# Four graph layers on 32 graphs: where the third and fourth graph's sums of scores are added up

## The chip, the cores and the metric

The kernel runs on one core of a Trainium2 chip. Its engines run side by side, each with its own queue of instructions in an order fixed at build time: PE (TensorE, matrix products into PSUM), DVE (VectorE), ACT (ScalarE), POOL (GpSimd) and SP, which here only issues transfers. They wait for one another by semaphores. The metric is the device time of one execution in microseconds (us), lower being better.

## The reference, cut to what matters

There are 32 graphs of 512 nodes with 128 features each, and one adjacency matrix (512 x 512, zeros and ones) for all of them. Four layers follow one another; each takes a layernorm with ReLU of x and adds its result to x. The change lies in the first, which per graph computes

```python
x_h = elu(x @ Wi + bi)
a_src = x_h @ We[:H, 0]
a_tgt = x_h @ We[H:, 0]
e = sigmoid(a_tgt[:, :, None] + a_src[:, None, :] + be[0])
e = e * (adj + ALPHA * (1.0 - (adj != 0)))
agg = einsum('bij,bjh->bih', e, x_h)
self_part = x_h * sum(e, axis=-1, keepdims=True)
recv = elu(concatenate([agg, self_part], axis=-1) @ Wn + bn)
out = concatenate([recv, x_h], axis=-1) @ Wm + bm
```

The sum over the last axis of e, here called the sum of scores, is one number for each of the 512 target nodes of a graph. The second layer is a recurrent one with five steps of gates, each with a product by the adjacency; the third multiplies by the adjacency and a weight; the fourth is a Chebyshev-like layer with three products by the adjacency for groups of four graphs.

## The kernel before, in words

A graph is held as four chunks of 128 nodes. In the first layer the scores are kept turned round, source nodes on the 128 partitions and the 512 target nodes along the row, so that they make four tiles `es[0]` to `es[3]`, one for each chunk of sources. ACT makes each as a tanh (line 619), and DVE adds one and multiplies by a mask (line 622). The message product (line 630) contracts each tile with the messages in a PSUM bank, `pn`.

The sum of scores is a sum over all four tiles and, inside a tile, over partitions, and it is wanted on all partitions. There are two ways in the code. For the graphs of the first group (b below G = 4) PE multiplies a matrix of ones (128 x 128, full fp32) with each of the four tiles and accumulates in a bank `ps` (line 637, by the helper `product`, whose matmul stands in line 441). For every later graph GpSimd adds the four tiles in three additions (line 641); ACT casts the sum to the reduced fp32r form, `high` (line 647); DVE forms what the cast left out, `low` (line 648); and PE multiplies ones, in fp32r, with both (line 653), into `ps`. After either way DVE multiplies `ps` with x_h (line 656), the product with the lower half of Wn is accumulated onto `pn`, and an elu, the output products (line 666) and the addition to x (line 461) follow. Then the second layer can begin: a layernorm (lines 473 to 486, with a power on GpSimd in line 478), and five steps (lines 839 to 876) of a product by the adjacency (line 820, split into a high and a low part made in lines 790 and 794), gates (lines 845 to 852) and the update (lines 862 to 866).

Besides the sums, graphs of the first group differ from later ones in how they are turned: they use PE transposes (lines 370 and 604), where later graphs go through DVE and transfers.

What sets the order is a planner, run when the kernel is built. Every operation is registered with an engine, an estimated duration, a due time, and what it reads and writes. `Plan.order` then deals them out as if on a clock: each engine takes the ready operation that is due first, provided that buffers are free and that it is due at most 60 us later than the oldest one not begun. An operation of DVE with two inputs in SBUF (`two=True`) and one of POOL never run at the same time in the plan. The resulting order is written into the queues. So an edit of one operation can move all that is planned after it. In the planner's books a full fp32 product is 0.86 us (`T_MM`), a pass of fp32r 0.23 us (`T_PASS`), an addition on GpSimd 1.6 us. A graph's dues count from `begin(b)`: 0, 14, 28 and 42 us for the first four graphs. The first 18 us are planned apart, up to a branch that chooses between exact and inexact adjacency; this adjacency is exact.

Buffers are in kinds: 36 tiles `f` in SBUF (128 x 512 fp32), 4 of fp32r `q`, 8 banks `b` of PSUM, and others.

Of the kernel before, what the change touches and what calls it, by code (L numbers as in the profile page):

```python
# [41 lines left out]
class Plan:  # L42
# [16 lines left out]
    def op(self, eng, us, due, emit, reads=(), writes=(), two=False, keep=0, result=None,  # L59
           earliest=0.0):  # L60

        o = Op(eng, us, self.RESULT[eng] if result is None else result, emit, two, keep)
        o.earliest = earliest
        for v in reads:
            o.before.add(v.writer)
        for v in writes:
            o.before.update(v.readers)  # L70
            if v.writer:
                o.before.add(v.writer)
            elif v.kind and v.slot is None:
                o.takes.append(v)
        for v in reads:
            v.readers.append(o)
        for v in writes:
            v.writer, v.readers = o, []
        o.vals = [v.whole or v for v in dict.fromkeys([*reads, *writes])]
        for v in o.vals:  # L80
            v.left += 1
        for v in [*reads, *writes, *o.vals]:
            self.vals[v] = True
        o.before -= {o, None}
        o.due = max([due, *(b.due for b in o.before)])
        for b in o.before:
            b.after.append(o)
        self.ops.append(o)
# [124 lines left out]
def tile_four_graph_layers(  # L213
# [30 lines left out]
    G = 4  # L244
# [32 lines left out]
    def at(v):  # L277
        if v.tile is not None:
            return v.tile
        return places[v.kind][v.slot] if v.whole is None else at(v.whole)[:, v.part]  # L280
# [152 lines left out]
    def product(w, src, due, dst=None, start=True, stop=True, blocks=False):  # L433

        dst = dst or Val("b")
        def emit():
            to, of = at(dst), at(src)
            if blocks:
                to = to.rearrange("p (c q i) -> p q c i", c=NC, i=32)
                of = of.rearrange("p (q c i) -> p q c i", c=NC, i=32)  # L440
            nc.tensor.matmul(to, at(w), of, start=start, stop=stop)  # L441
        op("PE", T_MM, due, emit, [src, w], [dst])
        return dst
# [104 lines left out]
    def layer0(b, h, due):  # L548
# [82 lines left out]
                at(pn), at(msg)[:, ts(jc, P)], at(es[jc]), start=jc == 0, stop=False),  # L631
                [msg, es[jc]], [pn])

        if b < G:
            ps = Val("b")
            for jc in range(NC):
                product(ones, es[jc], d, ps, start=jc == 0, stop=jc == NC - 1)
        else:
            sums = [Val("f"), Val("f")]
            def add(dst, a, c):  # L640
                op("POOL", 1.6, d - 10, lambda: nc.gpsimd.tensor_tensor(  # L641
                    at(dst), at(a), at(c), op=ALU.add), [a, c], [dst])
            add(sums[0], es[0], es[1])
            add(sums[1], es[2], es[3])
            add(sums[0], sums[0], sums[1])
            high, low, ps = Val("q"), Val("q"), Val("b")
            op("ACT", T_COPY, d, lambda: nc.scalar.copy(at(high), at(sums[0])), [sums[0]], [high])
            op("DVE", T_VEC, d, lambda: nc.vector.tensor_tensor(
                at(low), at(sums[0]), at(high).bitcast(F32), op=ALU.subtract),
                [sums[0], high], [low], two=True)  # L650
            def total():
                for n, part in enumerate((low, high)):
                    nc.tensor.matmul(at(ps), at(ones_r), at(part), start=n == 0, stop=n == 1)  # L653
            op("PE", 2 * T_PASS, d, total, [high, low, ones_r], [ps])
# [23 lines left out]
    def first_layer(b):  # L678
        h = layernorm(b, begin(b))
        layer0(b, h, begin(b))  # L680
# [316 lines left out]
```

## Time and profile before

| What | Value |
|---|---|
| median of 3 runs | 1689.95 us (1689.92 to 1690.58) |
| the profiled execution | 1689.17 us |
| its span (first to last instruction) | 1687.4 us |
| PE busy | 1667.7 us |
| DVE busy | 1457.7 us |
| ACT busy | 1127.8 us |
| POOL busy | 295.8 us |
| PE's products with ones | 32 records, 25.4 to 81.4 us |
| GpSimd's additions (line 641) | 84, of 1.55 us in the mean, 85.3 to 1384.6 us |
| PE's passes with ones in fp32r (line 653) | 56 records |

How to read it: a line of the profile names the kernel's line, the engine, the instruction, what it writes and reads, the shape and the count. A full fp32 matmul shows as two records; records of PE overlap in time, so their sum exceeds the time that passes. A view of stretches gives each engine's busy time between two moments of the span, then the granted clock, the transfer engines' share and GB/s. A view of waits gives for each pair of instructions the total, the count and the longest. The chain is the work that ended last, followed back from the end; its rows give a start, a duration and the work.

### The profile page before, as it was taken

How to read it: one execution, taken by the hardware profiler on the slowest of the kernel's cores; microseconds unless marked ns; L12 is line 12 of the kernel's file. 1: busy time of each engine (PE TensorE's matmuls, PEld its weight loads, DVE VectorE, ACT ScalarE, POOL GpSimd, SP SyncE). 2: the span in 40 equal slices, each digit the busy share in tenths (PEclk: the TensorE clock that was granted, in tenths of full speed). 3: DMA queues.
4: the chain of work that ended last, by engine and by line, in shares of the span. 5: the costliest groups of instructions: out<-in, count | busy, mean ns of one | idle time of the engine just before them, and what ended most of it. 6: DMA issues, size and time to landing. Idle time of an engine off the chain costs nothing.

```text
span 1687.4 us, 21306 instructions
## 1 busy us (share of the span) xinstructions
PE 1667.7 (99%) x6627; PEld 1076.8 (64%) x6627; DVE 1457.7 (86%) x3325; ACT 1127.8 (67%) x2143; POOL 295.8 (18%) x237
## 2 busy tenths in 40 slices
PE   9999999999999999999999999999999999999998
PEld 7555555656666666666666666666666666666797
DVE  6889999999998898889988898889999988877742
ACT  8777676786776676667776677665777766655541
POOL 2121102212122121222202212202222220000110
PEclk9999999999999999999999999999999999999999
DMA  3213333243333332242332433232333333222201
GB/s 107 62 57 101 94 107 94 78 135 95 101 113 101 101 101 85 84 120 95 105 103 77 112 107 92 90 107 88 118 104 99 97 98 94 82 69 88 83 18 52
DMA packets 266875, 156.57 MB, mean 93 GB/s; under 512 B 75392, under 2 KB 235008, under 8 KB 266752
## 3 DMA queue, kind: packets, MB, share of 16 engines
q1 hardware_dynamic: 266752, 155.12, 31.3%
q8 instruction: 54, 0.88, 0.2%
q14 instruction: 69, 0.57, 0.1%
HBM read 82.25 MB, written 72.81 MB: 92 GB/s over the span
## 4 chain that ended last, share of the span: by engine, by line
PE 89%; DVE 6%; ACT 2%; DMA 1%; issue 1%; SPq 0%; DVEq 0%; ACTq 0%
PE b L441 41%; PE b L820 19%; PE b L910 10%; PE b L901 6%; PE b L630 5%; PE b L666 3%; PE b L567 2%; PE b L883 1%; PE b L300 1%; DVE f L845 1%; DVE f L622 1%; DVE r L794 1%; PE b L653 1%; ACT f L486 1%; DVE f L382 1%
## 5 line engine op out<-in xcount | busy, mean ns | idle before, releaser
L478 POOL TENSOR_TENSOR s<-s,nhalf 128x4 f32<-128x4 f32 x128 | 160.0, 1250 | 884.4 <-DVE s L476 840.9
L430 ACT COPY f<-b 128x512 f32<-128x512 f32 x360 | 208.4, 586 | 158.7 <-PE b L820 107.1
L820 PE MATMUL b<-AQ,r 128*128 128x512 f32 x1024 | 302.5, 437 | 1.3 <-DVE r L794 1.3
L820 PEld LDWEIGHTS b<-AQ,r 128*128 128x128 f32 x1024 | 192.2, 188 | 89.9 <-issue 47.4
L845 DVE TENSOR_TENSOR f<-f,b 128x512 f32<-128x512 f32 x320 | 211.6, 676 | 39.8 <-PE b L441 39.1
L446 ACT ACTIVATE f<-f,b4w 128x512 f32<-128x512 f32 x160 | 115.4, 723 | 163.0 <-DVE f L845 160.5
L382 DVE STREAM_TRANSPOSE f<-f 128x512 f32<-128x512 f32 x244 | 205.2, 844 | 21.8 <-ACT f L486 21.3
L910 PE MATMUL b<-r,A_r 128*128 128x512 f32 x768 | 222.8, 426 | 0.0
L486 ACT ACTIVATE f<-x,s 128x128 f32<-128x128 f32 x512 | 210.8, 491 | 17.3 <-DVE s L481 17.2
L641 POOL TENSOR_TENSOR f<-f,f 128x512 f32<-128x512 f32 x84 | 129.9, 1548 | 427.0 <-DVE f L622 299.0
L441 PE MATMUL b<-f,u5T 128*128 128x512 f32 x320 | 163.4, 595 | 6.0 <-DVE f L852 6.0
L910 PEld LDWEIGHTS b<-r,A_r 128*128 128x128 f32 x768 | 139.4, 189 | 46.6 <-issue 24.4
L441 PE MATMUL b<-f,w4T 128*128 128x512 f32 x320 | 163.1, 593 | 2.5 <-ACT f L430 2.5
L441 PE MATMUL b<-f,u3T 128*128 128x512 f32 x320 | 163.3, 593 | 1.7 <-DVE f L866 1.6
L441 PE MATMUL b<-f,w5T 128*128 128x512 f32 x320 | 162.5, 592 | 0.0
L441 PE MATMUL b<-f,w3T 128*128 128x512 f32 x320 | 162.1, 592 | 0.0
L820 PE MATMUL b<-A_r,r 128*128 128x512 f32 x512 | 151.1, 437 | 0.4 <-DVE r L794 0.4
L901 PEld LDWEIGHTS b<-V,f 128*128 128x128 f32 x1024 | 131.8, 191 | 26.3 <-issue 20.1
L862 DVE TENSOR_TENSOR f<-f,f 128x512 f32<-128x512 f32 x160 | 112.9, 707 | 38.0 <-ACT f L446 37.7
L446 ACT ACTIVATE f<-b,b5w 128x512 f32<-128x512 f32 x160 | 109.1, 683 | 53.3 <-PE b L441 52.9
L794 DVE TENSOR_TENSOR r<-f,r 128x512 fp32r<-128x512 f32 x192 | 138.5, 723 | 6.4 <-ACT r L790 6.2
L446 ACT ACTIVATE f<-f,b3w 128x512 f32<-128x512 f32 x160 | 115.0, 720 | 28.8 <-DVE f L845 27.7
(106 smaller groups left out, 2580.5 us busy)
## 6 DMA issues: line engine op xcount, KB each, us to landing
m<-f SPq DMA_DIRECT2D x244, 256.0 KB, 2.1
f<-m SPq DMA_DIRECT2D x184, 256.0 KB, 2.9
f<-m SPq DMA_DIRECT2D x240, 64.0 KB, 2.3
x<-in_x_dram SPq DMA_DIRECT2D x32, 256.0 KB, 3.3
out_dram<-x SPq DMA_DIRECT2D x32, 256.0 KB, 2.4
f<-d SPq DMA_DIRECT2D x28, 256.0 KB, 5.6
f<-in_adj_dram SPq DMA_DIRECT2D x4, 256.0 KB, 3.8
f<-in_L_gnn_weight_dram SPq DMA_DIRECT2D x2, 224.0 KB, 3.3
```

The lines of the kernel that those rows point to most:

```text
L382: op("DVE", us, due, lambda: nc.vector.transpose(view_out(at(blocks)), view_in(at(src))), [src], [blocks])
L430: op("ACT", us, due, lambda: nc.scalar.copy(at(t), at(src)), [src], [t])
L441: nc.tensor.matmul(to, at(w), of, start=start, stop=stop)
L446: op("ACT", us, due, lambda: nc.scalar.activation(at(dst), at(src), AF.Tanh, bias=at(bias), scale=scale), [src, bias], [dst])
L478: op("POOL", 1.35, due, lambda: nc.gpsimd.tensor_tensor(stat(SCALE), stat(VAR), at(neg_half), op=ALU.pow), [s, neg_half], [s])
L486: nc.scalar.activation(at(h)[:, ts(c, P)], at(X[b])[:, c, :], AF.Relu, bias=stat(SHIFT)[:, c : c + 1], scale=stat(SCALE)[:, c : c + 1],)
L641: op("POOL", 1.6, d - 10, lambda: nc.gpsimd.tensor_tensor(at(dst), at(a), at(c), op=ALU.add), [a, c], [dst])
L794: op("DVE", T_VEC, due, lambda: nc.vector.tensor_tensor(part(lo), whole(), part(hi).bitcast(F32), op=ALU.subtract), [src, hi], [lo], two=two)
L820: nc.tensor.matmul(at(pa), at(part)[:, ts(jc, P)], view(at(columns)[:, jc, :]), start=jc == n == 0, stop=jc == NC - 1 and n == PARTS - 1,)
L845: op("DVE", T_VEC, d, lambda: nc.vector.tensor_tensor(at(s), at(u), at(pg), op=ALU.add), [u, pg], [s])
L901: nc.tensor.matmul(at(pz)[:, ts(i, D)], at(hT[i])[:, ts(ic, P)], at(V[k]), start=i == 0, stop=last and i == G - 1,)
L910: nc.tensor.matmul(at(pz), at(adjT)[:, jc, ts(ic, P)], at(part), start=False, stop=jc == NC - 1 and n == PARTS - 1,)
```

## The change

The condition that chooses between the two ways of summing is altered from `b < G`, with G = 4, to `b < 2`. The first and second graph keep the four fp32 products with ones; the third and fourth (b = 2 and 3) now use GpSimd's three additions, the cast, the subtraction and two fp32r passes. How these two graphs are turned, and everything else in the text of the program, stays as it is; the planner then deals out all operations anew.

```diff
-        if b < G:
+        if b < 2:
             ps = Val("b")
             for jc in range(NC):
                 product(ones, es[jc], d, ps, start=jc == 0, stop=jc == NC - 1)
```

## The prediction

> **What bounds the kernel now.** I read the page's busy shares first, then the busy time by stretches, PE's waits, and the rows of the instructions concerned. The shares:
>
> ```profile
> PE 1667.7 (99%) x6627; PEld 1076.8 (64%) x6627; DVE 1457.7 (86%) x3325; ACT 1127.8 (67%) x2143; POOL 295.8 (18%) x237
> ```
>
> PE is busy 99% of a span of 1687.4 us; DVE comes next. These are averages over unlike stages, so the busy times in stretches (PE, PEld, DVE, ACT, POOL, in us) follow. The products that the change removes lie in the second to fourth line:
>
> ```profile
> 40.00:60.00 20.00, 19.95 (x86) 12.25 (x85) 13.96 (x38) 15.61 (x32) 2.55 (x4) 1.00 0.15 49
> 60.00:80.00 20.00, 20.00 (x75) 11.47 (x74) 17.28 (x46) 15.97 (x31) 4.97 (x8) 1.00 0.24 67
> 80.00:100.00 20.00, 20.00 (x76) 11.93 (x75) 15.10 (x35) 16.42 (x32) 4.86 (x4) 1.00 0.18 54
> ...
> 100.00:200.00 100.00, 98.33 (x331) 56.54 (x330) 94.64 (x189) 70.43 (x128) 16.17 (x12) 1.00 0.30 92
> 200.00:300.00 100.00, 97.44 (x310) 54.90 (x309) 93.61 (x190) 65.91 (x121) 17.64 (x12) 1.00 0.29 91
> 300.00:400.00 100.00, 97.08 (x363) 59.42 (x362) 97.00 (x228) 76.49 (x148) 20.05 (x15) 1.00 0.39 111
> 400.00:500.00 100.00, 99.24 (x397) 64.37 (x396) 97.88 (x239) 72.30 (x142) 21.59 (x17) 1.00 0.36 106
> ```
>
> From 40 to 100 us PE has no gap to speak of and DVE is idle for 60 - 13.96 - 17.28 - 15.10 = 13.7 us. From 100 to 500 us the two are nearly level: PE loses 7.9 us there, and DVE is 94 to 98% busy. What PE waits for in all:
>
> ```profile
> PE b L441 <- DVE f L852: 6.0, 5, 1.8
> PE b L441 <- ACT f L430: 2.5, 3, 1.6
> PE b L820 <- DVE r L794: 1.7, 2, 1.3
> PE b L441 <- DVE f L866: 1.6, 1, 1.6
> PE b L300 <- DVE ones L295: 1.0, 1, 1.0
> PE b L630 <- DVE f L622: 0.6, 1, 0.6
> ```
>
> That is 13.4 us in 13 waits, for DVE and ACT alone, and 8.7 us of it (1.6 + 1.6 + 2.6 + 2.9 us by stretches of 100 us) lies between 0 and 400 us. So the end is set by PE's work, plus what the joint stretch makes PE wait. PE's part in the sums of scores, in its timeline and then in the chain that ended last (start, duration):
>
> ```profile
> 59.27 3.60 PE L441 MATMUL b<-f,ones 128*128 128x512 f32 x8
> ...
> 67.91 1.02 PE L441 MATMUL b<-f,ones 128*128 128x512 f32 x2
> ...
> 81.01 1.02 PE L441 MATMUL b<-f,ones 128*128 128x512 f32 x2
> ```
>
> ```profile
> 118.44 0.47 PE b L653 x2
> 118.91 3.43 PE b L441 x8
> ```
>
> The third graph's four products stand together at 59.27 us, the fourth's are scattered from 67.91 to 82 us (another two stand at 78.44 us); each is two records. Records of PE overlap (3.60 us here), so I take the step from the chain: eight records of such products pass in 3.43 us, 0.86 us a product. The pair of passes that later graphs use takes 0.47 us.
>
> **What the skill says.** "FP8 and Floating Point Precision", TensorE Precision Notes, counts four passes through the array for true fp32. The trace agrees in size: 0.86 us a product against 0.47 / 2 = 0.235 us for one reduced pass. "SBUF — State Buffer", Terms, calls the pair of ports that DVE and GpSimd arbitrate for an exclusive lock held for the whole instruction: the loser blocks fully. The trace agrees. In the DVE and POOL timelines, the scalar-tensor-tensor that usually takes 0.68 us takes 1.77 us beside an addition of GpSimd:
>
> ```profile
> 104.38 1.57 POOL L641 TENSOR_TENSOR f<-f,f 128x512 f32<-128x512 f32 x1 [7.95 <-PE b L441]
> ```
>
> ```profile
> 104.73 1.77 DVE L622 SCALAR_TENSOR_TENSOR f<-f,mask 128x512 f32<-128x512 f32 x1
> ```
>
> "Perfetto Trace Analysis", Identifying the Most-Contended Engine, warns that matmul busy share is a poor measure of the distance to the roofline. Here I use it only for gaps: what counts is that no gap follows the removed products.
>
> **The change part by part.**
>
> *Removed from PE:* 2 graphs x 4 products x 0.86 = 6.9 us. *Added to PE:* 2 graphs x 0.47 = 0.9 us. Net 5.9 us less, all of it on the chain that ended last, since PE has no gap from 60 to 140 us.
>
> *Added to GpSimd:* 6 additions x 1.55 us (mean of the row of line 641) = 9.3 us. POOL is busy 7.5 us of 40 to 80 us and stands idle for 9.85 us ahead of 60.02 us and 14.85 us ahead of 78.65 us. The third graph's scores (line 622) are done at 49.6 us; its additions fit there. The fourth's are made at 65.39, 66.59, 69.60 and 70.80 us; two additions can follow the last of them by 74.5 us. A power of a layernorm (line 478, 1.25 us) can come to stand behind one addition, so up to 1.6 us late, and then DVE's line 481 with it. Line 481 waited 1.4 us for POOL in the whole run, so I take nothing for this. The cover is the planner's dealing with several graphs at once; without it the price is 1.6 us a time.
>
> *Added to ACT:* 2 casts x 0.62 = 1.2 us; ACT is idle for 8.4 us between 40 and 80 us. In 28 graphs the cast (line 647) waited 0.5 us in all for POOL, so little queues behind it.
>
> *Added to DVE:* 2 subtractions x 0.69 = 1.4 us, and the lock. The lock's price: lines 622, 852, 862, 864, 866 and 794 have means 203, 21, 27, 24, 16 and 43 ns over 680 ns; times 128, 4 x 160 and 192 instructions these are 26 + 14 + 8 = 48 us. Put on the 84 additions alone, it is 0.58 us each, so 6 x 0.58 = 3.5 us. Its bounds are nothing (GpSimd falls on instructions that read PSUM) and the whole addition, 9.3 us. I take 3.5, which makes 4.9 us on DVE, between 1.4 and 10.7. It is hidden by DVE's 13.7 us of idleness between 40 and 100 us. But PE, 5.9 us ahead, wants DVE's results that much sooner: 4.9 + 5.9 = 10.8 of 13.7 us are then used, and not all idle time can be used. I charge 1 us to this. If the cover were gone, the whole 4.9 us would be paid.
>
> *The waits of the new path:* cast, subtraction, pair of passes, and line 656 behind them. In 28 graphs line 648 waited 2.2 us for ACT and line 656 3.3 us for PE, 0.2 us a graph, in DVE's queue. Against this, the sum is known earlier: the third graph's last score is done at 49.6 us, while its line 656 ran at 62.9; the fourth's ran at 82.5. Nothing that I see becomes late. *Buffers:* two more of the 36 f buffers a graph for a few us, two of 4 q buffers that were last used for the adjacency casts; and a PSUM bank held about 1.5 us, where the fourth graph held one from 67.9 to 83.2 us. No price, perhaps a small gain. *DMA:* no transfer is added, removed or issued elsewhere on purpose; SP's queue changes only by its order.
>
> *The order:* the planner writes all queues from about the first such addition on anew, with 4 x 0.86 us of PE replaced by 2 x 0.23 in its books, and each addition keeping two-input work of DVE away for 1.6 us. The work after 100 us is the same, in another order, and so meets other waits. PE's loss in stretches of 100 us is 1.7, 2.6, 2.9, 0.8 and 1.6 us between 100 and 600 us, then 0 to 1.5. An estimate from this scatter, about 1 us a stretch over 16 stretches: the sum of 13.4 us can come out 4 us higher or lower. It can't fall below 0, so no more than 5.9 + 13.4 = 19 us can be won.
>
> Sum against the profiled execution (1689.17 us; span 1687.4): 1689.17 - 5.9 + 1.0 = 1684.2. The median of the runs, 1689.95, is 0.8 us above the profiled one, so 1685.0 us.
>
> **The rivals.** 0.2% of 1690 us is 3.4 us, about what a measurement can tell from no change.
>
> *A. Won, as summed.* 1681 to 1686.5 us, at 1685. For it: PE's closed row from 60 to 140 us. Against it: the level race after 100 us.
>
> *B. The gain waits at DVE.* PE comes to the stretch from 100 to 500 us up to 5.9 us early, and DVE can't follow: PE's waits grow from 13.4 to 17 or 19 us. At 146 us PE did wait, and the chain ran over DVE and ACT for 13 us. Time about 1689, between 1686.5 and 1693.3. Against it: DVE's idle time before 100 us, much of it spent waiting for PE, which now comes sooner.
>
> *C. DVE starts the stretch late: slower.* Place: lines 622 and 542 to 866 between 48 and 80 us, held by the lock. Price: up to 10.7 us on DVE, all PE's gain then lost in waits behind it. It decides from the point where the idle time takes up less than 10.7 - 3.4 = 7.3 us at the upper price (less than 1.5 of 4.9 at the middle one). Typical: 5 us unpaid, 1695; worst 1690 + 10.7 = 1700.7. For it: two-input work fills most of DVE's queue from 64 to 71 us. Against it: 13.7 us of idleness.
>
> *D. A luckier order.* Waits fall too: under 1681 us.
>
> That the additions aren't made at all is no case: the branch is taken at build time by graph number.
>
> **How the numbers follow.** A 0.42, D 0.06, B 0.27, C 0.25. Faster by over 0.2% is A and D, 0.48; within it B, 0.27; slower C, 0.25. Likeliest: A, 1685, with its own range 1681 to 1686.5. The range for 8 in 10 leaves out about 0.04 of D under 1679 and a little under half of C, 0.11, over 1696: 1679 to 1696.
>
> **What would show it.** Records of products with ones fall from 32 to 16, line 641 rises from 84 to 90, line 653's records from 56 to 60. PE's share stays at 99% and its waits within 13 +- 4 us, if A holds. B would show waits of PE for DVE between 100 and 500 us some 4 to 6 us longer; C would show DVE busy for more than 52 of the 60 us from 40 to 100 us (46.3 now, 51.2 as summed), and the rows of lines 622 and 852 to 866 longer there. The forecast is wrong if the new order makes PE lose more than 2.5 us over the 13.4, or if DVE's rows before 100 us lengthen by more than 5 us.

## The result, and the profile after

The changed kernel took 1685.13 us in the median of 9 runs (1684.39 to 1687.89), against 1689.95 us before (9 runs, 1689.15 to 1690.65). The ratio is 0.9972, with a 95% interval of 0.9962 to 0.9983: 4.8 us faster. The forecast was 1685.0 us. The profiled execution took 1684.65 us (1689.17 before).

The busy shares of the changed kernel, and then what PE waited for:

```profile
PE 1663.9 (99%) x6615; PEld 1073.5 (64%) x6615; DVE 1467.1 (87%) x3327; ACT 1129.3 (67%) x2145; POOL 308.0 (18%) x243
```

```profile
PE b L441 <- DVE f L852: 6.0, 9, 1.2
PE b L630 <- DVE f L622: 2.7, 2, 2.0
PE b L820 <- DVE r L794: 1.1, 2, 0.7
PE b L653 <- DVE q L648: 1.1, 3, 0.7
PE b L300 <- DVE ones L295: 1.0, 1, 1.0
PE b L441 <- ACT f L430: 0.5, 1, 0.5
```

The waits sum to 12.4 us (13.4 before), inside the 13 +- 4 us of the forecast. PE has 12 records fewer: 16 records of products with ones (two for each of eight products) are gone and 4 passes came. POOL has 6 instructions more, DVE and ACT two each. So far all is as summed. But the waits have moved, as the busy times in stretches show. First before, then after:

```profile
0.00:100.00 100.00, 98.27 (x456) 64.37 (x457) 73.54 (x218) 81.05 (x166) 22.26 (x39) 1.00 0.28 79
100.00:600.00 500.00, 490.47 (x1783) 298.51 (x1782) 471.94 (x1033) 349.28 (x659) 94.88 (x68) 1.00 0.33 99
600.00:1300.00 700.00, 697.68 (x2750) 450.06 (x2749) 628.98 (x1446) 482.49 (x921) 135.60 (x98) 1.00 0.34 100
1300.00:1600.00 300.00, 300.00 (x1141) 191.75 (x1140) 251.78 (x552) 186.48 (x342) 38.63 (x28) 1.00 0.29 86
```

```profile
0.00:100.00 100.00, 94.30 (x446) 61.57 (x447) 78.82 (x218) 82.27 (x168) 33.20 (x46) 1.00 0.27 79
100.00:600.00 500.00, 498.57 (x1826) 306.14 (x1825) 473.65 (x1068) 356.73 (x676) 102.98 (x69) 1.00 0.34 101
600.00:1300.00 700.00, 695.32 (x2731) 446.46 (x2730) 633.78 (x1429) 481.69 (x916) 132.31 (x98) 1.00 0.33 99
1300.00:1600.00 300.00, 298.97 (x1146) 191.36 (x1145) 250.93 (x538) 184.72 (x341) 35.10 (x27) 1.00 0.29 88
```

Before 100 us PE is idle for 5.7 us where it was 1.7. From 100 to 600 us it is idle for 1.4 us where it was 9.5. After 600 us it loses some 3.4 us more. These differences are as large as the gain, so the right total says little about why. PE's timeline of the changed kernel between 60 and 84 us shows where most of the early time went:

```profile
60.32 0.72 PE L653 MATMUL b<-q,ones_r 128*128 128x512 f32 x2
...
63.37 1.13 PE L441 MATMUL b<-f,Wn_sb 128*128 128x512 f32 x2
66.52 2.33 PE L630 MATMUL b<-f,f 128*128 128x512 f32 x4 [2.03 <-DVE f L622]
...
82.41 1.12 PE L441 MATMUL b<-f,u5T 128*128 128x512 f32 x2 [1.24 <-DVE f L852]
...
83.83 1.03 PE L653 MATMUL b<-q,ones_r 128*128 128x512 f32 x2
```

The pairs for the third and fourth graph stand at 60.32 and 83.83 us. PE comes to the fourth graph's messages at 64.2 us and finds no score ready (it waits 2.03 us for line 622). Later it waits 1.24 us for line 852, the state of the second layer multiplied by a gate, which the product with the weight u5 reads.

To compare runs I use one measure. From the trace of before I take the usual step from one PE instruction to the next for each kind (0.43 us for half a full fp32 product of 512 columns, 0.23 for an fp32r pass, and so on). PE's work is the sum of these steps; *lost time* is what the starts lie apart beyond them. Each of the 14 profiled executions is then work + lost time + 6.4 to 6.8 us behind the last start. For before this is 1663.6 + 16.3 + 6.4, and with the 1.0 us before PE's first instruction it comes to the span of 1687.4 within a few tenths; for after it is 1657.6 + 17.6 + 6.5. Lost time is slightly above the idle time of the stretches, as overlapping records hide a little. The columns of lost time below belong to the one profiled execution of each kernel, which lies up to 1.7 us off that kernel's median (o1 1.6 us above, e6 1.7 us below, before 0.8 us below), so differences of a us or two between rows are within that scatter.

| Kernel | Median us | PE's work, to before | lost 0 to 100 us | lost after 100 us |
|---|---|---|---|---|
| before | 1689.95 | 0 | 3.6 | 12.7 |
| after | 1685.13 | -5.9 | 9.0 | 8.6 |
| e1, before's order, less PE | 1688.14 | -5.2 | 7.1 | 13.3 |
| e2, after's order, PE restored | 1690.39 | -0.3 | 8.6 | 8.2 |
| e3, fourth graph alone | 1692.24 | -3.0 | 5.2 | 17.0 |
| e4, second graph too | 1696.01 | -8.9 | 12.4 | 19.1 |
| o1, before, other order (1.5) | 1690.99 | 0 | 3.8 | 15.7 |
| o2, before, other order (1.7) | 1690.01 | 0 | 3.7 | 12.5 |
| o3, after, other order (1.5) | 1685.38 | -5.9 | 8.8 | 8.6 |
| o4, after, other order (1.7) | 1687.80 | -5.9 | 9.2 | 11.1 |
| e5, less PE, planned | 1689.45 | -5.2 | 4.3 | 16.7 |
| e6, additions and products | 1697.10 | 0 | 4.4 | 18.0 |
| e7, fourth alone (1.5) | 1688.89 | -3.0 | 4.1 | 15.7 |
| e8, fourth alone (1.7) | 1691.94 | -3.0 | 6.7 | 15.4 |

The change took 5.9 us of work from PE, of which 5.4 us came back as lost time before 100 us; at 100 us the kernel was 0.5 us ahead. The rest, 4.1 us of the 4.6 us between the two profiled spans, is lost time that no longer occurs after 100 us. The experiments ask whether the removed work or the new order of the queues earned it.

### The profile page after: what moved, and what is told of

Same layout as the page of the kernel before. It is cut to its first block, busy times and chain, and to the rows that moved or that the text cites. A ratio compares the mean times of both kernels' runs of the same rounds, so it can differ in the third digit from the quotient of the medians.

```text
span 1682.8 us, 21311 instructions
## 1 busy us (share of the span) xinstructions
PE 1663.9 (99%) x6615; PEld 1073.5 (64%) x6615; DVE 1467.1 (87%) x3327; ACT 1129.3 (67%) x2145; POOL 308.0 (18%) x243
## 4 chain that ended last, share of the span: by engine, by line
PE 81%; DVE 9%; ACT 2%; DMA 2%; issue 1%; SPq 0%; DVEq 0%; ACTq 0%
PE b L441 38%; PE b L820 18%; PE b L910 10%; PE b L901 6%; PE b L630 3%; PE b L666 3%; DVE f L622 2%; PE b L883 1%; PE b L567 1%; DVE r L794 1%; DVE f L845 1%; DVE f L382 1%; DMA f<-d 1%; PE b L653 1%; DVE f L852 1%
## 5 line engine op out<-in xcount | busy, mean ns | idle before, releaser
L478 POOL TENSOR_TENSOR s<-s,nhalf 128x4 f32<-128x4 f32 x128 | 155.2, 1213 | 817.9 <-DVE s L476 775.3
L641 POOL TENSOR_TENSOR f<-f,f 128x512 f32<-128x512 f32 x90 | 146.1, 1626 | 479.3 <-DVE f L622 323.3
L910 PE MATMUL b<-r,A_r 128*128 128x512 f32 x768 | 226.8, 430 | 0.0
L901 PEld LDWEIGHTS b<-V,f 128*128 128x128 f32 x1024 | 131.0, 191 | 24.4 <-issue 19.1
```

Source lines behind the costliest of these rows:

```text
L478: op("POOL", 1.35, due, lambda: nc.gpsimd.tensor_tensor(stat(SCALE), stat(VAR), at(neg_half), op=ALU.pow), [s, neg_half], [s])
L641: op("POOL", 1.6, d - 10, lambda: nc.gpsimd.tensor_tensor(at(dst), at(a), at(c), op=ALU.add), [a, c], [dst])
L901: nc.tensor.matmul(at(pz)[:, ts(i, D)], at(hT[i])[:, ts(ic, P)], at(V[k]), start=i == 0, stop=last and i == G - 1,)
L910: nc.tensor.matmul(at(pz), at(adjT)[:, jc, ts(ic, P)], at(part), start=False, stop=jc == NC - 1 and n == PARTS - 1,)
```

## Experiments

Two theories. W: the time follows PE's work, with the order as noise. O: the gain comes from the new order, and the removed work itself would have been lost in waits. The medians of before in the three series were 1689.38 (e1 to e4), 1689.37 (o1 to o4) and 1689.87 us (e5 to e8); each ratio is to its own series.

### e1: the old order, with less work of PE

```diff
-                product(ones, es[jc], d, ps, start=jc == 0, stop=jc == NC - 1)
+                op("PE", T_MM, d, lambda: None, [es[jc], ones], [ps]) if b >= 2 and jc < NC - 1 else product(ones, es[jc], d, ps, start=jc == 0 or b >= 2, stop=jc == NC - 1)
```

> The kernel before with its order kept: of the four fp32 products with ones of the third and of the fourth graph, three each are planned but not issued (6 x 0.86 = 5.2 us of PE's work gone; the sums of these two graphs lack three of four tiles). All other instructions, and their order on every engine, are those of before. Theory W (the time follows PE's work): 1690.0 - 5.2 = 1684.8 us, at most 1.5 us more. Theory O (what is won comes from the new order, and less work of PE under the old order only waits longer for VectorE between 100 and 600 us): 1688 to 1690 us, with PE's waits of 13 us grown by 3 to 5 us.

Measured: 1688.14 us, ratio 0.9993 (0.9986 to 1.0000). Of 5.2 us of removed work 1.2 us was won, so W fails for this order. The loss lies before 100 us (7.1 against 3.6 us), not between 100 and 600 us where O had put it; the lost time after 100 us is that of before (13.3 and 12.7). Where PE was when the products had gone, first in the timeline of before, then of e1:

```profile
59.27 3.60 PE L441 MATMUL b<-f,ones 128*128 128x512 f32 x8
62.71 1.02 PE L441 MATMUL b<-f,u5T 128*128 128x512 f32 x2
...
78.44 1.88 PE L441 MATMUL b<-f,ones 128*128 128x512 f32 x4
80.15 1.02 PE L441 MATMUL b<-f,u5T 128*128 128x512 f32 x2
```

```profile
59.41 1.02 PE L441 MATMUL b<-f,ones 128*128 128x512 f32 x2
61.34 1.12 PE L441 MATMUL b<-f,u5T 128*128 128x512 f32 x2 [0.91 <-DVE f L852]
...
75.23 1.88 PE L630 MATMUL b<-f,f 128*128 128x512 f32 x4
78.39 1.12 PE L441 MATMUL b<-f,u5T 128*128 128x512 f32 x2 [1.28 <-DVE f L852]
```

In the old order products with ones stand just ahead of a product with u5, which needs the gated state that ACT and DVE form in the meantime (tanh, then line 852). They filled that wait. The trace of before had the margin: line 852 ended at 61.1 and 79.1 us, only 1.6 and 1.1 us ahead of the two u5 products. e1 takes three products (2.6 us) away ahead of the first and two (1.7 us) ahead of the second, and what goes beyond the margins comes out as waits, 0.91 and 1.28 us. A gap-free PE hid a second chain of nearly the same length.

### e2: the new order, with PE's work put back

```diff
-                for n, part in enumerate((low, high)):
+                for n, part in [(0, low), (1, high)] * (7 if b < G else 1):
```

> The changed kernel with its order kept: the pair of fp32r passes of the third and of the fourth graph is issued seven times in place of once, each time started afresh, so that 2 x 6 x 0.47 = 5.6 us of PE's work come back, nearly what the change took away. Theory W: 1685.1 + 5.6 = 1690.7 us, less at most 2 us that fall into waits of PE before 100 us. Theory O: 1685 to 1687 us, as PE had room under the new order.

Measured: 1690.39 us, ratio 1.0007 (1.0000 to 1.0014), 5.3 us above the changed kernel. Here 5.6 us of work cost nearly all of it, as W says, although 9 us are lost before 100 us. Only a little of the work falls into those waits. It stands ahead of line 656 of its own graph and delays DVE too: the third graph's line 656 moved from 62.63 to 64.19 us, and the fourth graph's first score (line 622) from 65.78 to 67.42 us (0.3 us of it was there before the added work), so PE's wait for that score shrank only from 2.03 to 0.95 us, and new waits came behind it. e1 and e2 agree in one thing: with the order kept, 5 us of PE's work more or less leave the lost time after 100 us as it is (12.7 and 13.3; 8.6 and 8.2). That part goes with the order of the queues.

### e3 and e4: one graph, and three

```diff
-        if b < G:
+        if b < 3:
             ps = Val("b")
```

e4 has `b < 1`.

> Half of the change: only the fourth graph takes GpSimd's additions (b < 3). Theory W: half of PE's saving, 1690.0 - 3.0 + 0.5 = 1687.5 us, with 4 us on either side for the new order. Theory O: no relation to the work; anywhere from 1684 to 1692 us.

> One graph more: the second graph takes GpSimd's additions as well (b < 1). Theory W: 1690.0 - 8.9 of PE's work + 2 us for VectorE and the lock = 1683 us, with 4 us on either side for the new order. Rival: between 20 and 40 us ScalarE is busy 20.0 of 20 us, so the cast comes late and PE waits before 60 us: 1686 us or more, with waits of PE before 100 us of over 10 us (9.0 in the changed kernel).

Measured: e3 1692.24 us, ratio 1.0016 (1.0009 to 1.0023); e4 1696.01 us, 1.0035 (1.0022 to 1.0048). Both have less work on PE than before, and both are slower. e4's rival was right on the early waits, 12.4 us, but most of its loss lies later, at 19.1 us. In e3 most lies later (17.0 us), and PE's waits between 200 and 300 us make up 5.2 us of it:

```profile
PE b L630 <- DVE f L622: 3.5, 1, 3.5
PE b L441 <- DVE f L852: 1.7, 1, 1.7
```

### o1 to o4: other orders of the same instructions

```diff
-                op("POOL", 1.6, d - 10, lambda: nc.gpsimd.tensor_tensor(
+                op("POOL", 1.5, d - 10, lambda: nc.gpsimd.tensor_tensor(
```

o1 and o2 are the kernel before with 1.5 and 1.7 in the planner's books, o3 and o4 the changed kernel. Nothing is computed otherwise; all queues are dealt anew.

> The kernel before with one number in the planner's books altered, an addition of GpSimd taken as 1.5 us in place of 1.6. Not one instruction is added or removed; the order alone becomes another. If the order counts for little (the prediction's 4 us on either side): 1686 to 1694 us, most likely within 2 us of 1690. If what the changed kernel won lies within what any new order can win or lose: a difference of 4 us or more in at least one of these two runs of the kernel before.

> The same with 1.7 us in the planner's books. Theory of little order: within 2 us of 1690. Theory of the order: 4 us or more away in one of the two, to either side.

> The changed kernel with 1.5 us in the planner's books, the order alone being another. Theory W (PE's removed work is what was won): within 2 us of 1685. Theory of the order: the gain isn't kept; about 1690 with 4 us on either side, since the removed products only filled waits of PE before 100 us.

> The changed kernel with 1.7 us in the planner's books. Theory W: within 2 us of 1685. Theory of the order: about 1690 with 4 us on either side; the means of the three orders of each kernel (1.5, 1.6, 1.7) differ by less than 3 us.

Measured: o1 1690.99 us, ratio 1.0012 (1.0003 to 1.0020); o2 1690.01, 1.0004 (0.9996 to 1.0013); o3 1685.38, 0.9978 (0.9968 to 0.9988); o4 1687.80, 0.9990 (0.9983 to 0.9997). So O falls in its strong form: the gain isn't the luck of one order. W holds for o3, but o4 lies 2.8 us above its 1685 us. The three orders of before have a mean of 1690.3 us, those of after 1686.1, and they don't overlap; neither kernel has an order 4 us away from its first. Three orders of each are few, but in them the early loss hardly depends on the order (3.6 to 3.8 before, 8.8 to 9.2 after), and the later one is lower in each order of after (8.6 to 11.1) than in any of before (12.5 to 15.7), also when each is set right for the distance of its execution from the median (9 to 12 against 13 to 14).

### e5 and e6: each part of the change by itself

e5 leaves three products of each of the two graphs out of the plan too:

```diff
-                product(ones, es[jc], d, ps, start=jc == 0, stop=jc == NC - 1)
+                product(ones, es[jc], d, ps, start=jc == 0 or b >= 2, stop=jc == NC - 1) if b < 2 or jc == NC - 1 else None
```

e6 keeps all products and puts the additions, casts and subtractions beside them, without the fp32r passes, so that nothing waits for the sums:

```diff
                 product(ones, es[jc], d, ps, start=jc == 0, stop=jc == NC - 1)
+            if b >= 2:
+                sums = [Val("f"), Val("f")]
+                ...
+                add(sums[0], es[0], es[1])
+                add(sums[1], es[2], es[3])
+                add(sums[0], sums[0], sums[1])
+                high, low = Val("q"), Val("q")
+                ...
```

> Three of the four products with ones of the third and of the fourth graph are neither issued nor planned (6 x 0.86 = 5.2 us of PE's work gone, and the planner knows it; no addition of GpSimd, cast or subtraction in their place, so the sums of these two graphs lack three of four tiles). If the freed time of PE is used once the planner may fill it: 1684.8 us, waits of PE before 100 us near 4 us. If the other engines' chain sets the pace before 100 us: 1688 to 1690 us less what the new order gives or takes, waits of PE before 100 us at 7 us or more.

> The kernel before with the six additions, two casts and two subtractions of the third and fourth graph put in beside the products with ones, which stay; their results aren't used. PE's work is that of before. If the additions and the lock cost PE nothing (the prediction: hidden, 1 us at most): waits of PE before 100 us 4 to 5 us, 1690 us with 3 us on either side for the order. If it is they that made PE wait in the changed kernel: waits before 100 us of 7 us or more, 1693 us or more.

Measured: e5 1689.45 us, ratio 1.0000 (0.9991 to 1.0009); e6 1697.10, 1.0047 (1.0030 to 1.0063). In e5 the planner does fill the freed time (4.3 us lost before 100 us), so at 100 us PE is 4.5 us ahead; then it loses 16.7 us instead of 12.7, and little is left. So the freed time was used early, as the first expectation had it, but the total was not the 1684.8 us that goes with it. Nor is it rival B as the prediction placed it, between 100 and 500 us. The busy times of e5:

```profile
100.00:600.00 500.00, 491.54 (x1796) 299.45 (x1795) 470.28 (x1045) 349.96 (x661) 94.62 (x68) 1.00 0.34 100
600.00:1300.00 700.00, 696.09 (x2729) 446.78 (x2728) 629.52 (x1439) 483.72 (x920) 134.65 (x99) 1.00 0.34 99
```

From 100 to 600 us PE is idle for 8.5 us, less than the 9.5 of before; from 600 to 1300 us it is idle for 3.9 us where before had 2.3.

In e6 the additions cost PE only 0.8 us before 100 us, well covered, as the prediction had it, and 5.3 us afterwards. The two parts alone give -0.4 and +7.2 us, the change -4.8: the parts don't add up. Each alone, in the one order that was run, loses 17 to 18 us after 100 us; the change loses 9 to 11 in three.

### e7 and e8: the fourth graph alone, in other orders

```diff
-        if b < G:
+        if b < 3:
...
-                op("POOL", 1.6, d - 10, lambda: nc.gpsimd.tensor_tensor(
+                op("POOL", 1.5, d - 10, lambda: nc.gpsimd.tensor_tensor(
```

e8 has 1.7.

> Only the fourth graph takes the additions, with 1.5 us for an addition in the planner's books, so in another order. If its loss (1692.2 us) was a bad order: 1687 to 1689 us, waits of PE after 100 us of 8 to 13 us in place of 17. If it belongs to the cut itself: 1691 to 1693 us.

> The same with 1.7 us in the planner's books. Bad order: 1687 to 1689 us. The cut itself: 1691 to 1693 us.

Measured: e7 1688.89 us, ratio 0.9994 (0.9985 to 1.0002); e8 1691.94, 1.0009 (1.0002 to 1.0016). The order moves this cut by 3.3 us, and its mean over three orders, 1691.0 us, is no better than before's, with 15.4 to 17.0 us lost after 100 us. The expectations split: e7 took the time of the bad order, though not its smaller waits, and e8 that of the cut itself. A bad order explains part of e3, but in none of the three orders was the saving of PE won.

What stays open: why the cut at 2 loses so much less after 100 us than those at 4, 3 and 1. It isn't PE's lead at 100 us, which is 0.5 us in the changed kernel and 4.5 us in e5, the one with 16.7 us of losses. It isn't one lucky order either, by o3 and o4. How the graphs stand to one another when they enter the stretch in which DVE and PE are level would be a reason, but no run isolates it.

## Why the prediction was right, and where it was not

**The total** was 1685.0 and is 1685.1 us; the case was A, and the range holds it. That it agrees to 0.1 us is luck: one term came out far larger than summed, and another, put at zero, nearly made up for it.

**PE's work:** summed at 5.9 us less; it is 1663.6 - 1657.6 = 5.9 us. Right.

**"All of it on the chain that ended last":** this step failed. That PE has no gap says only that it was never seen waiting, not that its work could be taken away with profit. e1 removed 5.2 us and won 1.2. The prediction asked what happens "if the cover were gone" for DVE's added work only; it should have asked it of the removed products too, which were themselves the cover of the u5 product's wait.

**"Hidden by DVE's 13.7 us of idleness, 1 us charged":** the term measured 5.4 us before 100 us, five times its size. DVE's busy time between 40 and 100 us went from 46.33 to 51.65 us, against 51.2 as summed:

```profile
40.00:100.00 60.00, 55.98 (x224) 33.01 (x223) 51.65 (x117) 48.88 (x96) 23.22 (x23) 1.00 0.18 57
```

This agrees, but it doesn't prove the size: a new order also brings other work into the stretch, and e5, with none of the additions, shows 50.83 us there. Up to 100 us DVE's busy time rose by 5.3 us (73.54 to 78.82), just over the 5 us that the prediction named as a sign of being wrong, if busy time stands for its "rows".

Idle time is no store to draw on: between 40 and 100 us of before all of DVE's gaps but 0.3 us were waits for PE and ACT, and they stand where the fixed order puts them. With the queues planned anew, neither the additions alone (e6, 0.8 us) nor the saving alone (e5, 0.7 us) cost much there; both at once cost 5.4. With the old order kept, the saving alone cost 3.5 (e1). The chain that ended last shows the path: from 60 to 100 us it runs over PE alone in before and in e5, but in the changed kernel over DVE from 65.7 to 82.4 us. Part of it, in the changed kernel:

```profile
73.55 2.88 DVE f L622 x3
76.44 1.15 DVE s L481
...
82.41 1.12 PE b L441 x2
```

**The lock** showed as forecast, here on the instruction of DVE that stood beside the fourth graph's addition (POOL and DVE timelines of after):

```profile
67.81 1.60 POOL L641 TENSOR_TENSOR f<-f,f 128x512 f32<-128x512 f32 x1 [2.14 <-PE b L630]
```

```profile
68.19 1.76 DVE L542 SCALAR_TENSOR_TENSOR f<-f,f 128x512 f32<-128x512 f32 x1
```

1.76 us where 0.69 is usual. At 73.48 us three instructions of line 622 took 2.96 us in all beside the next addition, where such instructions follow one another every 0.60 us, and at 76.36 us line 481 took 1.22 us in place of 0.16. These three delays, about 3 us, lie on the chain above, which ends in PE's wait of 1.24 us; for a late line 481 the prediction took nothing. But the lock isn't the whole cause. Just before PE's longer wait, of 2.03 us, DVE's work took its usual times, and DVE came late because it had been busy without a gap from 55.7 us on. And o3 loses as much before 100 us (8.8 us), while its chain runs over transfers and ACT from 66 to 82 us.

**"The sum is known earlier":** only just for the third graph (line 656 at 62.63 us, 62.91 before), and not for the fourth (84.90, 82.54 before), since ACT took up its cast at 81.44 us and DVE its subtraction at 82.88 us, though GpSimd had finished the additions by 78.8 us.

**The order:** put at 4 us either way. The orders of one cut lie 1 to 3.3 us apart, so the size holds. But it was treated as noise around PE's saving. In fact 4.1 us of the 4.6 us between the profiled executions came from losses after 100 us that are lower in every order of the changed kernel, for a reason that stays open. The forecast's 1 us of net loss was really +5.4 and -4.1.

**The rivals:** B, with its waits between 100 and 500 us, didn't come about: from 100 to 600 us PE's idle time fell from 9.5 to 1.4 us. C came about in part: PE's longest waits for DVE before 100 us stand behind the lines that it named, with the lock on the path to one of them, and nearly all of the saving was lost in time of this kind; DVE's 51.65 us stayed just under its sign of 52. Only the lower losses after 100 us kept the total at A. e6, slower by 7.2 us, isn't C either, as its losses lie after 100 us.

## What to carry to other kernels

An engine that shows no gap may still not be what bounds the kernel: when two chains run level, each fills the other's waits. Removing work from one then pays only as far as the other can follow. Ask of every piece of work to be removed what stands behind it waiting for something else, and read from the trace how long before its start that was ready: here 1.6 and 1.1 us, which was about what could be won there in that order. Then test it with the order kept. Where a planner rewrites the queues, run each variant in two or three orders before the difference is put down to the edit.

## What the runs showed of the hardware

Nothing that contradicts what the prediction used. A full fp32 product passes in 0.86 us and a pair of fp32r passes in 0.47 us in both kernels, and GpSimd's additions held DVE's two-input instructions up by about one microsecond where they met (1.76 us in place of 0.69), even the small ones of line 481 (1.22 us in place of 0.16). What such a delay costs isn't a property of the addition: in e6 PE lost 0.8 us before 100 us, in the changed kernel, with the same additions and less work on PE, 5.4 us.
